# A state-space scan whose sums over states are issued one step later, with a guard on the order of the scans and a closed-up group of gelus

## The chip, the cores and the metric

The kernel runs on one core of one Trainium2 chip. The metric is the device time of one execution in microseconds; of several runs the median is taken. Smaller is better.

## The reference, cut to what matters

The kernel computes a chain of eight blocks over 2048 tokens of width 128 (8 sequences of 256), each followed by a layer norm. The change touches the stage that holds the second and third blocks: a local-attention layer (two sub-layers, each with attention and a gated feed-forward) and a selective state-space layer ("mamba") behind it. What it computes, for a sequence:

```
# gated feed-forward of a local sub-layer
h = h @ w1 + b1
a, g = split(h, 2)
x = x + (a * gelu(g)) @ w2 + b2

# state space: 256 inner channels, 16 states each
dA  = exp(delta[..., None] * A)                 # decay per step, channel and state
dBx = delta[..., None] * B[:, :, None, :] * xc[..., None]
h_t = dA_t * h_(t-1) + dBx_t                    # a scan along the 256 tokens
y_t = sum over the 16 states of h_t * C_t       # the sum over states
y   = (y + xc * D) * silu(z)
out = y @ W_out
```

## The kernel before, in words

Activations lie with channels on the 128 partitions and tokens along the free dimension. The method `local_mamba` holds the stage. Its work is written as Python generators, one for each sequence: `one_sequence` runs the two local sub-layers (`local_block`, with `local_attention` and `local_qk` inside), and `mamba_sequence` follows for the same sequence. A generator yields a number, its nominal length, and `interleave` always continues the one whose running sum is smallest. Four local sequences are open at a time, started 24 units apart; up to two mamba sequences run beside them, started at least 20 units apart. So the order in which the instructions are written down is a merge of up to six streams.

That order isn't yet the order on an engine. The framework that builds the program takes the place in the written order as a priority and lets each engine's next instruction be the one of highest priority among those that it reckons ready at that point. Whatever comes out is then fixed, and each engine takes its instructions in that order: in this trace TensorE stands idle for 42.9 us in front of sums over states that wait for VectorE, whatever is queued behind them. Two helpers bend the order: `issue_after` makes one instruction come behind another on the same engine, with no wait for its end; `wait_for` makes one wait for the end of another. `exp_ln` puts a load of the activation table for exp and ln behind the last activation written so far.

The steps that the change concerns:

- The scan (`mamba_sequence`, L776 to L793). A sequence has 8 steps, each with two of the 16 states. For each step, ScalarE makes the decay `da` by four exps (L785). VectorE multiplies `u` by the broadcast rows of B into `hs` (L787), scans (L789) and multiplies by the broadcast rows of C (L790). All three are 128x1024 in float32. Then TensorE adds the two states into the PSUM bank `yp` with two float32 matmuls of 128x512 against the identity (L792); a float32 matmul is two records in the profile, so a step has four. The program's name for `yp` is `y`. The buffers `hs` and `bc` (the broadcast rows, loaded by SyncE's queue, L754) have three slots each, `yp` has one.
- The end of a sequence (L794 to L802): VectorE reads `yp` (L796), GpSimd multiplies by silu(z) (L797; in the last sequence VectorE does), and TensorE applies `W_out`.
- The gate of the feed-forward (`local_block`, L685 to L694): three pairs of matmuls into the PSUM tiles `g`, then three gelus on ScalarE (L693), then `exp_ln`. Gelu lies in another activation table than exp and ln.
- The last sequence's mamba runs with other work woven in (`among`, `beside`): weight loads for the next stages, foldings of attention weights on TensorE (`fold`), and the routing of the next stage.

Of the kernel before, what the change touches and what calls it, by code (L numbers as in the profile page):

```python
# [15 lines left out]
AF = mybir.ActivationFunctionType  # L16
# [5 lines left out]
P = 128  # L22
# [274 lines left out]
class _Kernel:  # L297
    def __init__(self, ctx, tc, ins, out):
        self.tc, self.nc, self.ins, self.out = tc, tc.nc, ins, out
        nc = self.nc  # L300
        pool = lambda name, bufs=1, **kw: ctx.enter_context(tc.tile_pool(reuse_waits="tile", name=name, bufs=bufs, **kw))
        self.pool = pool


        self.right = lambda name, scope=ctx, bufs=1: scope.enter_context(
            tc.tile_pool(reuse_waits="tile", name=name, bufs=bufs, side="right")
        )
        self.const = const = pool("const")
        self.xs = pool("xs", 2)
        self.dram = pool("dram", space=DRAM)  # L310
        self.tags = {}


        self.chunk_scope = ctx.enter_context(ExitStack())
        self.tail = ctx.enter_context(ExitStack())
        self.scope = ctx.enter_context(ExitStack())
        n = ins["w0"].shape[1] // 2
        self.w0 = self.right("w0", self.scope).tile([P, 2, n], F32, name="w_local")
        self.x = self.xs.tile([P, T], F32, tag="x", name="x_in")
        nc.sync.dma_start(self.x, ins["x"])  # L320
        self.c12 = const.tile([P, 2], F32, name="c12")
        self.zero = const.tile([P, 1], F32, name="zero")
        nc.gpsimd.memset(self.zero, 0.0)
        self.one = const.tile([P, 1], F32, name="one")
        nc.gpsimd.memset(self.one, 1.0)
        self.wg = const.tile([P, 2, P], F32, name="wg")
        nc.sync.dma_start(self.wg, ins["wg"].rearrange("p (a b) -> p a b", a=2))
        self.vec = const.tile([P, _V["n"]], F32, name="vec")
        nc.sync.dma_start(self.vec, ins["vec"])
        self.rot = const.tile([P, 512], F32, name="rot_table")  # L330
        nc.sync.dma_start(self.rot, ins["cst"][:, slice(*_C["rot"])])
        r = slice(_C["iota32"][0], _C["n"])
        self.rt = const.tile([P, r.stop - r.start], F32, name="route_tables")
        nc.sync.dma_start(self.rt, ins["cst"][:, r])
        self.msk = const.tile([P, _M["n"]], BF, name="msk")
        nc.gpsimd.dma_start(self.msk, ins["msk"])
        self.ident = const.tile([P, P], F32, name="ident")
        make_identity(nc, self.ident)
        self.centre = const.tile([P, P], F32, name="centre")
        nc.vector.tensor_scalar(self.centre, self.ident, -1.0 / P, None, ALU.add)  # L340
        self.identb = const.tile([P, P], BF, name="identb")
        nc.vector.tensor_copy(self.identb, self.ident)
        self.mean = const.tile([P, P], F32, name="mean")
        nc.gpsimd.memset(self.mean, 1.0 / P)

        self.lg1 = [const.tile([P, n, 32], F32, name=f"lg1{n}") for n in (14, 2)]
        self.lg2 = const.tile([P, NT, 8], F32, name="lg2")
        self.ssq = const.tile([P, NT], F32, name="ssq")

        self.put1 = const.tile([P, NT], I32, name="put1")  # L350
        self.get1 = const.tile([P, NT], I32, name="get1")
        self.gate1 = const.tile([P, NT], F32, name="gate1")
        self.sum1 = const.tile([P, 32], BF, name="sum1")

        self.put2 = const.tile([P, 2, NT], I32, name="put2")
        self.get2 = const.tile([P, 2, NT], I32, name="get2")
        self.gate2 = const.tile([P, 2, NT], F32, name="gate2")
        self.sum2 = const.tile([P, 8], BF, name="sum2")
        self.onesb = const.tile([P, P], BF, name="onesb")
        nc.gpsimd.memset(self.onesb, 1.0)  # L360
        for l in range(2):
            nc.sync.dma_start(self.w0[:, l, :], ins["w0"][:, l * n : (l + 1) * n])
        self.w1 = const.tile([P, ins["w1"].shape[1]], F32, name="w1")
        nc.sync.dma_start(self.w1, ins["w1"])

        self.places = [self.dram.tile([2560, P], F32, name=f"places{i}") for i in range(2)]
        self.scatters = [], []
# [23 lines left out]
        return self.ps.tile([P, n], F32, tag=tag, name=name, bufs=self.tags[tag])  # L391

    def mm(self, out, lhsT, rhs, start=True, stop=True):
        return self.nc.tensor.matmul(out, lhsT, rhs, start=start, stop=stop)  # L394

    def issue_after(self, later, earlier):

# [268 lines left out]
    def local_block(self, l, x, w, rot, work, local, small, pools):  # L666

        nc = self.nc
        wo = w[:, l, 1536:2048].rearrange("p (c f) -> p c f", c=4)
        w1 = w[:, l, 2048:2730]  # L670
        w2 = w[:, l, 2730:3114].rearrange("p (c f) -> p c f", c=3)
        h = local.tile([P, S], F32, tag="h", name="h", bufs=3)
        self.shift(h, x)
        yield 1.0
        ot = yield from self.local_attention(l, h, w, rot, work, local, small, pools)
        ps = self.psum("M", "wo")
        for c in range(4):
            self.mm(ps[:, 0:S], wo[:, c, :], ot[:, c, :], c == 0, c == 3)
        x2 = local.tile([P, S], F32, tag="x2", name="x2", bufs=3)
        nc.vector.tensor_add(x2, ps[:, 0:S], x)  # L680
        h2 = work.tile([P, S], F32, tag="h2", name="h2")
        self.shift(h2, x2)
        yield 2.5
        self.layernorm(work, h2, h2)
        yield 4.5  # L685
        ge = local.tile([P, 3, S], F32, tag="ge", name="ge")
        size = lambda c: min(P, 341 - c * P)
        gs = [self.psum("M", "g") for _ in range(2)]
        part = lambda c: gs[c // 2][0 : size(c), c % 2 * S : (c % 2 + 1) * S]
        for c in range(3):  # L690
            self.mm(part(c), w1[:, 341 + c * P : 341 + c * P + size(c)], h2)
        for c in range(3):
            last = nc.scalar.activation(ge[0 : size(c), c, :], part(c), AF.Gelu, bias=self.v(f"b1g{l}", c)[0 : size(c), :])  # L693
        self.exp_ln(last)  # L694
        yield 4.0
        ps = self.psum("M", "a")
        for c in range(3):
            m = size(c)
            a = ps[0:m, c * S : (c + 1) * S] if c < 2 else gs[1][0:m, S : 2 * S]
            self.mm(a, w1[:, c * P : c * P + m], h2)  # L700
            nc.vector.scalar_tensor_tensor(ge[0:m, c, :], a, self.v(f"b1a{l}", c)[0:m, :], ge[0:m, c, :], ALU.add, ALU.mult)
        yield 2.0
        ps = self.psum("M", "w2")
        for c in range(3):
            m = size(c)
            self.mm(ps[:, 0:S], w2[0:m, c, :], ge[0:m, c, :], c == 0, c == 2)
        x3 = local.tile([P, S], F32, tag="x3", name="x3", bufs=3)
        nc.vector.scalar_tensor_tensor(x3, ps[:, 0:S], self.v(f"b2{l}"), x2, ALU.add, ALU.add)
        yield 1.5
        return x3  # L710


    def mamba_sequence(self, b, x, y, na, das, work, scan):


        nc = self.nc
# [56 lines left out]
        u = tile("u", 2)  # L773
        eng.tensor_mul(u, d, xc)  # L774
        yield 3.0
        yp = self.psum("Y", "y")  # L776
        shp = [P, 2, 2, S]
        for m in range(8):
            bc = rows(m)
            bn, cn = (bc[:, k].unsqueeze(2).to_broadcast(shp) for k in range(2))  # L780
            da = das[m % len(das)]
            for n in range(2):
                for c in range(2):
                    i = 16 * c + 2 * m + n
                    nc.scalar.activation(da[:, n, c, 1:S], d[:, c, 1:S], AF.Exp, scale=na[:, i : i + 1])  # L785
            hs = scan.tile(shp, F32, tag="hs", name="hs", bufs=3)
            nc.vector.tensor_tensor(hs, u.unsqueeze(1).to_broadcast(shp), bn, ALU.mult)  # L787
            line = lambda a: a.rearrange("p n c s -> p (n c s)")
            nc.vector.tensor_tensor_scan(line(hs), line(da), line(hs), 0.0, ALU.mult, ALU.add)  # L789
            nc.vector.tensor_tensor(hs, hs, cn, ALU.mult)  # L790
            for n in range(2):
                self.mm(yp, self.ident, flat(hs[:, n]), m == 0 and n == 0, m == 7 and n == 1)  # L792
            yield 2.3  # L793
        yg = tile("t")  # L794
        for c in range(2):
            nc.vector.scalar_tensor_tensor(yg[:, c, :], xc[:, c, :], self.v("dpar", c), yp[:, c * S : (c + 1) * S], ALU.mult, ALU.add)  # L796
        eng.tensor_mul(yg, yg, sz)  # L797
# [1015 lines left out]
```

## Time and profile before

| what | us |
|---|---|
| median of 3 runs | 1901.54 |
| lowest and highest | 1899.53, 1904.87 |
| the profiled execution: its time | 1852.0 |
| the profiled execution: its span | 1850.2 |
| mean granted TensorE clock in it | 0.929 |
| busy over the span: TensorE | 1557.4 (84%) |
| busy over the span: VectorE | 1095.6 (59%) |
| busy over the span: ScalarE | 1028.5 (56%) |
| busy over the span: GpSimd | 563.7 (30%) |

The first scan of the stage starts at 279.7 us and the last ends at 903.5 us; the stage's local attention begins before it, from about 100 us, and the next stage's gathers follow from about 925 us. The profile's rows give line, engine, operation, output and inputs by the program's names, the shape, the number of instructions, then busy time and mean duration in ns, and after the second bar the time that the engine stood idle just before these instructions, with what ended it. L394 is the helper that records all matmuls, so matmuls are told apart by their tiles. PE is TensorE, PEld its weight loads, DVE VectorE, ACT ScalarE, POOL GpSimd, SPq the queue of SyncE.

### The profile page before, as it was taken

To read this page: it belongs to the slowest core of one execution; us is meant where nothing else is said; L and a number is where in the kernel's file an instruction comes from. 1 tells how busy PE (TensorE), PEld (TensorE's weight loads), DVE (VectorE), ACT (ScalarE), POOL (GpSimd) and SP (SyncE) were. 2 spreads that over 40 slices of the span, in tenths; PEclk is the share of its full clock that TensorE was granted. 3 is DMA by queue.
4 is the path that set the end of the run, shared out by engine and by line. 5 is a ranking of instruction groups with operands and counts; after the bars stand their busy time and mean duration, and the time that the engine had idled before them with its cause. 6 is when DMAs were issued, how large, how long until landed. Compare 5 with 4: busy or idle time off the path is not lost.

```text
span 1850.2 us, 28438 instructions
## 1 busy us (share of the span) xinstructions
PE 1557.4 (84%) x10810; PEld 942.1 (51%) x10810; DVE 1095.6 (59%) x2016; ACT 1028.5 (56%) x2704; POOL 563.7 (30%) x493
## 2 busy tenths in 40 slices
PE   3668987878787867777579999999997999899997
PEld 2234543544454434344266766667663654465554
DVE  5734557777777776868714445557444223567664
ACT  4557776776777785566224454445443223465654
POOL 1324443433343323210511111111112025355552
PEclk7799998989998998788779999999998999899998
DMA  4000012111212121246440000000101311000000
GB/s 177 1 1 1 1 36 57 36 46 24 70 22 64 47 53 46 57 149 202 119 117 10 5 10 7 7 4 3 39 3 31 77 52 32 1 4 5 7 4 10
DMA packets 58330, 75.51 MB, mean 41 GB/s; under 512 B 5869, under 2 KB 35237, under 8 KB 57169
## 3 DMA queue, kind: packets, MB, share of 16 engines
q1 hardware_dynamic: 52864, 67.57, 12.8%
q0 software_dynamic: 3216, 5.07, 1.0%
q8 instruction: 85, 1.39, 0.3%
q10 hardware_dynamic: 2112, 1.05, 0.2%
q14 instruction: 53, 0.43, 0.1%
HBM read 65.46 MB, written 9.71 MB: 41 GB/s over the span
## 4 chain that ended last, share of the span: by engine, by line
PE 54%; DVE 19%; ACT 13%; issue 6%; POOL 6%; DMA 2%; POOLq 0%; DVEq 0%; SPq 0%; ACTq 0%
PE vps L394 7%; PE sc L394 7%; PE kps L394 6%; DVE hs L789 4%; PE out L394 4%; PE pt L475 4%; PE o L394 3%; PE pu L394 3%; PE pg L394 3%; ACT e L647 3%; DVE hs L790 2%; DVE hs L787 2%; PE y L394 2%; PE acc L394 2%; PE py L394 2%
## 5 line engine op out<-in xcount | busy, mean ns | idle before, releaser
L394 PE MATMUL y<-hs,ident 128*128 128x512 f32 x256 | 147.6, 706 | 42.9 <-DVE hs L790 42.8
L789 DVE TENSOR_TENSOR_SCAN hs<-da,hs 128x1024 f32<-128x1024 f32 x64 | 148.7, 2331 | 3.8 <-ACT da L785 3.3
L475 PE MATMUL pt<-ident,e 128*128 128x128 f32 x768 | 124.5, 288 | 28.2 <-POOL e L652 18.8
L1682 ACT ACTIVATE e<-sc,nm 128x128 f32<-128x128 f32 (+1 forms) x256 | 104.2, 424 | 59.3 <-DVE nm L1677 58.9
L652 POOL TENSOR_TENSOR e<-e,rc 128x1024 f32<-128x1024 f32 x32 | 72.2, 2255 | 204.6 <-DVE rc L651 204.5
L785 ACT ACTIVATE da<-d,na 128x255 f32<-128x255 f32 x256 | 112.1, 501 | 37.1 <-DVE hs L789 18.7
L1685 POOL TENSOR_TENSOR e<-e,rc 128x1024 f32<-128x1024 f32 x48 | 92.0, 1917 | 127.2 <-DVE rc L1684 94.2
L647 ACT ACTIVATE e<-sc,nm,rn 128x128 f32<-128x128 f32 x256 | 113.5, 464 | 25.2 <-DVE nm L642 25.0
L475 PEld LDWEIGHTS pt<-ident,e 128*128 128x128 f32 x768 | 89.2, 145 | 70.9 <-POOL e L652 25.4
L599 POOL TENSOR_TENSOR t<-t,t 128x512 f32<-128x512 f32 x64 | 89.1, 1392 | 96.5 <-DVE t L586 85.6
L1294 POOL TENSOR_TENSOR e<-e,rc 128x512 f32<-128x512 f32 x32 | 33.6, 1053 | 274.6 <-DVE rc L1293 160.3
L787 DVE TENSOR_TENSOR hs<-u,bc 128x1024 f32<-128x1024 f32 x64 | 86.6, 1362 | 43.2 <-POOL u L774 28.1
L394 PEld LDWEIGHTS y<-hs,ident 128*128 128x128 f32 x256 | 52.1, 219 | 98.9 <-DVE hs L790 55.7
L1269 ACT COPY kp<-kps 128x512 f32<-128x512 f32 x128 | 74.9, 585 | 42.2 <-PE kps L394 41.7
L477 ACT COPY ptsb<-pt 128x512 f32<-128x512 f32 x89 | 52.2, 587 | 82.4 <-PE pt L475 80.7
L1118 POOL DMA_INDIRECT got<-ybuf,get x48 | 45.7, 951 | 157.5 <-DMA ybuf<-ys 116.5
L394 PE MATMUL qk<-w_local,h 128*128 128x512 f32 x128 | 72.4, 653 | 17.6 <-DVE t L586 13.0
L477 DVE COPY ptsb<-pt 128x512 f32<-128x512 f32 x103 | 69.1, 685 | 29.8 <-PE pt L475 29.6
L790 DVE TENSOR_TENSOR hs<-hs,bc 128x1024 f32<-128x1024 f32 x64 | 81.8, 1286 | 0.2
L1677 DVE TENSOR_REDUCE nm<-sc 128x4 f32<-128x1024 f32 (+1 forms) x48 | 58.6, 1221 | 24.1 <-PE sc L394 23.9
L394 PE MATMUL sc<-km,q 64*128 64x512 f32 x192 | 69.9, 648 | 1.7 <-DVE FunctionType.Silu _12235 L1500 0.9
L1242 DVE BATCH_NORM_STATS2 st<-out 128x6 f32<-128x128 f32 x80 | 20.0, 288 | 81.0 <-PE out L394 74.0
(394 smaller groups left out, 3843.4 us busy)
## 6 DMA issues: line engine op xcount, KB each, us to landing
bc<-xs SPq DMA_DIRECT2D x128, 256.0 KB, 4.7
w_attn<-in_w_dram SPq DMA_DIRECT2D x4, 1024.0 KB
w_local<-in_w_dram SPq DMA_DIRECT2D x2, 1557.0 KB
places<-zeros SPq DMA_DIRECT2D x2, 1280.0 KB
w_moe<-in_e1gate_dram SPq DMA_DIRECT2D x8, 256.0 KB
w_moe<-in_e1up_dram SPq DMA_DIRECT2D x8, 256.0 KB, 7.5
w_moe<-in_e1down_dram SPq DMA_DIRECT2D x8, 256.0 KB, 5.3
w_moe<-in_e2rg_dram SPq DMA_DIRECT2D x8, 256.0 KB
```

What stands on the lines that cost most here:

```text
L394: return self.nc.tensor.matmul(out, lhsT, rhs, start=start, stop=stop)
L475: self.last = self.nc.tensor.transpose(pt[:, j * P : (j + 1) * P], src[:, j * P : (j + 1) * P], self.ident)
L477: self.nc.any.tensor_copy(sb.rearrange("p a b -> p (a b)"), pt)
L599: nc.gpsimd.tensor_add(t1, t1, t2)
L647: nc.scalar.activation(e[:, j, g, :], scs[:, j, g, :], AF.Exp, bias=nm[:, j, g : g + 1], scale=rq[:, j, g : g + 1], accum_out=sm[:, j, g : ...
L785: nc.scalar.activation(da[:, n, c, 1:S], d[:, c, 1:S], AF.Exp, scale=na[:, i : i + 1])
L787: nc.vector.tensor_tensor(hs, u.unsqueeze(1).to_broadcast(shp), bn, ALU.mult)
L789: nc.vector.tensor_tensor_scan(line(hs), line(da), line(hs), 0.0, ALU.mult, ALU.add)
L790: nc.vector.tensor_tensor(hs, hs, cn, ALU.mult)
L1269: nc.scalar.copy(k[:, 2 * i : 2 * i + 2, :].rearrange("p a b -> p (a b)"), ps)
L1682: nc.scalar.activation(e[:, i, :], sc[:, i, :], AF.Exp, bias=nm[:, i : i + 1], accum_out=sm[:, i : i + 1])
L1685: nc.gpsimd.tensor_tensor(e, e, rc.unsqueeze(2).to_broadcast([P, n, keys]), ALU.mult)
```

## The change

There are three edits.

1. The two summing matmuls of a step aren't written behind their own step. They are kept in a deque, and written after the following step's three VectorE instructions. Each is put behind the matmul that was written last before that point, by whichever stream (`self.pe_last`, which `mm` now records). The last step's sums come right after the loop. A step's nominal length becomes 2.5 in place of 2.3.
2. A guard: a sequence's scan doesn't begin to be written until the scan of the sequence before it is all written (`self.scanned`); until then the generator yields 0.5 at a time.
3. The three gelus are written at high priority, and the first of them waits for the end of the last of the three pairs of matmuls.

```diff
@@ __init__
+        self.scanned = 0
@@ mm
-        return self.nc.tensor.matmul(out, lhsT, rhs, start=start, stop=stop)
+        self.pe_last = self.nc.tensor.matmul(out, lhsT, rhs, start=start, stop=stop)
+        return self.pe_last
@@ local_block
         for c in range(3):
-            self.mm(part(c), w1[:, 341 + c * P : 341 + c * P + size(c)], h2)
-        for c in range(3):
-            last = nc.scalar.activation(ge[0 : size(c), c, :], part(c), AF.Gelu, bias=self.v(f"b1g{l}", c)[0 : size(c), :])
+            m = self.mm(part(c), w1[:, 341 + c * P : 341 + c * P + size(c)], h2)
+
+        with self.tc.high_priority():
+            for c in range(3):
+                last = nc.scalar.activation(ge[0 : size(c), c, :], part(c), AF.Gelu, bias=self.v(f"b1g{l}", c)[0 : size(c), :])
+                if c == 0:
+                    self.wait_for(last, m)
         self.exp_ln(last)
@@ mamba_sequence
+        while self.scanned < b:
+            yield 0.5
         yp = self.psum("Y", "y")
+        summed = deque()
+
+        def add(i, hs, last):
+
+            for n in range(2):
+                j = self.mm(yp, self.ident, flat(hs[:, n]), i == 0 and n == 0, i == 7 and n == 1)
+                self.issue_after([j], last)
@@ the loop over the 8 steps
             nc.vector.tensor_tensor_scan(line(hs), line(da), line(hs), 0.0, ALU.mult, ALU.add)
             nc.vector.tensor_tensor(hs, hs, cn, ALU.mult)
-            for n in range(2):
-                self.mm(yp, self.ident, flat(hs[:, n]), m == 0 and n == 0, m == 7 and n == 1)
-            yield 2.3
+            summed.append((m, hs))
+            last = self.pe_last
+            if m:
+                add(*summed.popleft(), last)
+            yield 2.5
+        add(*summed.popleft(), self.pe_last)
         yg = tile("t")
+        self.scanned = b + 1
```

## The prediction

> **What bounds the kernel now.** I read the busy time by stretches first: scans beside full local attention (280 to 760 us), the thinning end (760 to 850), the last scan nearly alone (850 to 910). Columns: length, busy us (instructions) of PE, PEld, DVE, ACT, POOL, then the granted PE clock, DMA share, GB/s.
>
> ```profile
> 280.00:760.00 480.00, 376.91 (x1955) 214.45 (x1955) 366.64 (x437) 354.50 (x872) 174.77 (x149) 0.93 0.20 48
> 760.00:850.00 90.00, 65.94 (x288) 37.70 (x290) 66.84 (x69) 43.73 (x98) 15.23 (x9) 0.83 0.44 138
> 850.00:910.00 60.00, 40.84 (x181) 21.40 (x179) 48.87 (x59) 27.83 (x61) 20.57 (x14) 0.83 0.56 171
> ```
>
> In the first stretch PE, DVE and ACT are 79%, 76% and 74% busy: none is full. They pass work to each other, so what counts is who stands waiting for whom. In the last, DVE is at 81% and leads. Next, the costliest groups of the page:
>
> ```profile
> L394 PE MATMUL y<-hs,ident 128*128 128x512 f32 x256 | 147.6, 706 | 42.9 <-DVE hs L790 42.8
> L789 DVE TENSOR_TENSOR_SCAN hs<-da,hs 128x1024 f32<-128x1024 f32 x64 | 148.7, 2331 | 3.8 <-ACT da L785 3.3
> ...
> L787 DVE TENSOR_TENSOR hs<-u,bc 128x1024 f32<-128x1024 f32 x64 | 86.6, 1362 | 43.2 <-POOL u L774 28.1
> ...
> L790 DVE TENSOR_TENSOR hs<-hs,bc 128x1024 f32<-128x1024 f32 x64 | 81.8, 1286 | 0.2
> ```
>
> The sums over states (y) make PE wait 42.9 us for the multiply by C (L790). A step costs DVE 2.33+1.36+1.29 = 4.98 us, 64 of them 319 us. PE's waits from 280 to 850 us, where other work is queued behind the sums:
>
> ```profile
> PE y L394 <- DVE hs L790: 31.2, 24, 3.5
> PE pt L475 <- POOL e L652: 14.5, 5, 7.9
> PE ln L394 <- POOL h L563: 11.8, 8, 2.2
> ```
>
> The sums are PE's largest wait; the other 11.7 us lie after 850, where PE has little else to do. Then the chain of waits, 280 to 800 us, its pieces of y:
>
> ```profile
> 316.46 3.78 PE y L394 x4
> ...
> 399.50 3.67 PE y L394 x4
> ...
> 578.14 3.78 PE y L394 x4
> 593.54 3.28 PE y L394 x4
> ```
>
> The same view gives DVE's three hs lines 12.1%, 7.0% and 5.8% of these 520 us, y 5.5%. So the chain runs through DVE's scans far more than through PE. Of the 24 waits it passes only five: by PE's timeline 2.65, 2.96, 3.31, 1.29 and (at 788.49) 0.22 us. Last, a gelu triple on ACT:
>
> ```profile
> 383.87 1.28 ACT L693 ACT_TABLE_LOAD   x1
> 385.17 0.47 ACT L693 ACTIVATE ge<-g,vec 128x256 f32<-128x256 f32 x1
> 385.66 1.28 ACT L593 ACT_TABLE_LOAD   x1
> 386.95 0.22 ACT L593 ACTIVATE rn<-rn 128x16 f32<-128x16 f32 x1
> 387.19 1.28 ACT L693 ACT_TABLE_LOAD   x1
> 388.48 0.47 ACT L693 ACTIVATE ge<-g,vec 128x256 f32<-128x256 f32 x1
> ```
>
> An exp slips between two gelus, and the table is loaded twice more. L693 has 22 loads for 16 triples: six such splits, 12 extra loads.
>
> **What the Trainium skill says.** "TensorE: Matmul & The Clock Gate", in the section on the array's 16 sub-arrays: PE can pull weight loads ahead, but matmuls start strictly in order. The trace agrees: a waiting y leaves PE idle whatever is behind it. The same page, Part 1, says that the clock halves after an idle window; here a y matmul takes 592 ns as a median and 1222 at most. "ScalarE: Activation LUTs", What ACT_TABLE_LOAD costs: 1283 ns and about 1380 ns of drain. The trace has the 1283 ns; the next activation follows within 0.02 us, and the load starts 0.02 us after the gelu, so I count no drain. "DVE: opcode table, instruction layouts, handler registers and perf-mode slots", Datapath: a scan runs at half throughput; here 2331 ns against 1286 for a multiply of that size. The change leaves that cost alone.
>
> **The sums one step later.** Nothing is removed: 256 matmuls and their weight loads stay. The moved step issues no DMA and passes no queue but PE's; `bc` is released by L790, so SP's loads are untouched. A sum now comes behind the matmul written last before the following step's position. Steps stand about 7.1 us apart (in the third sequence 472.1 to 528.9 us, 8 steps), so hs is normally finished. All 31.2 us of waits can go at most. I credit what the chain passes: 2.65+2.96+3.31+1.29+0.22 = 10.4 us. The others end in slack: the chain at those times is in DVE, whose queue still carries 4.98 us a step. The four long groups shown also run at the slow clock: 3.78+3.67+3.78+3.28 less 4 x 1.98 (the group at 788.49) is 6.6 us. A sum that follows running work should be warm, but the next wait may cool other matmuls: I take half, 3.3, with ends 0 and 6.6. After 850 us the wait isn't credited: DVE is late next. The last sum of a sequence still comes straight after its multiply, so the final `t` waits as now (3.71 us in the last sequence). The 2.5 in place of 2.3 gives each step a slightly lower priority against the local streams: unknown, see the noise below.
>
> **The guard.** By adding up the yields: mamba sequences begin 23 or 24 units apart, a scan starts 8 units in and lasts 8 x 2.5 = 20, so it is over (28) before the next one's starts (31). No 0.5 is ever yielded. The trace agrees: the first sequence's last scan starts at 331.9 us, the second's first at 376.4. Cost and gain nothing; there is no cover that could go.
>
> **The gelus.** High priority and the common start close the six splits: 12 x 1.283 = 15.4 us of ACT. On the chain lies one, the one shown: 2 x 1.283 = 2.6 us. The others are behind ACT's slack. The added wait: the first gelu holds ACT's queue (exps of attention and of `da`, whose waiters are DVE's) until the third pair of g. Four matmul records took 1.03 us at 482.99, so 16 triples cost 0 to 16 us. I take 0: the order is laid out with the gelus when g should be ready, and the last gelu is no later than now. Below zero it can't go, apart from the loads already counted.
>
> **Noise of the order.** Every shift re-sorts the queues. From 629 to 658 us, a silu placed behind the combined exp/ln table cost a row of single loads (L592, L593, L766, L785, L439 among them), some 11 until the table returned at 674.9: 14 us of ACT. Another order may lose or repeat it: minus 14 to plus 14, taken as 0.
>
> **Sum.** 10.4 + 3.3 + 2.6 = 16.3 us off the profiled execution's 1852.0, 0.88%. The median of the runs shown is 2.7% above that execution, so I scale: 1901.5 x (1 - 16.3/1852.0) = 1884.8, say 1885.
>
> **Rivals.** *All of it counts:* 31.2 + 15.4 = 46.6 us, 1901.5 x (1 - 46.6/1852) = 1853.7. For it: the three engines are equally loaded, so each stall may come back. Against: five of 24 waits on the chain.
>
> *Nothing comes of it:* DVE's queue holds everything, and PE merely waits elsewhere: 1901.5. For it: 25% of the chain is hs on DVE. Against: DVE itself waits 57.9 us for PE between 280 and 850.
>
> *Slower, by the slots of hs:* there are three, and the multiply by B (L787) of step m needs the sum of step m-3 done. That now ends later in PE's order. I took each sum's end (less its wait) one step later and compared it with the end of the multiply by C before the step in need: of 40 cases the median slack is 3.8 us, three are short, by 13.2 us together. If PE runs another 2 us behind, 13 are short, by 26.6; at 3 us 18, by 41.8. The loss overtakes the gain of 16.3 at about 0.5 us beyond a full step. At 2 us: 26.6 - 16.3 = 10.3 more, 1901.5 x (1 + 10.3/1852) = 1912. For it: only 2.3 us of L787's waits are on y now, but often just 2 us after the slot came free. Against: a sum can go a step late at most where PE is that far behind the written order.
>
> **Chances.** The forecast 0.52, all of it 0.16, nothing 0.10, slower 0.22. About 0.3% (5.7 us) is what a measurement can tell from no change. Faster 0.68, same 0.10, slower 0.22. The forecast alone, with its bounds (clock, gelu wait, noise), spans 1868 to 1900. The range reaches into both outer cases: 1855 to 1912, leaving out half of each.
>
> **What would show it.** Right: y's wait on L790 between 280 and 850 us falls under 8 us; L693 has 16 loads; first and last scans keep their order; L787 waits little for y. The last scan (867 to 905) keeps its length. Wrong: L787 idle for y by over 15 us (slots), PE's total idle unchanged with other names on it (nothing), or new rows of table loads.

## The result and the profile after

| | before | after |
|---|---|---|
| median us (7 runs each) | 1903.64 | 1916.57 |
| ratio, 95% interval | | 1.0072 [1.0057, 1.0086] |
| profiled execution, its span in us | 1850.2 | 1917.0 |
| start of the first scan, us | 279.7 | 285.9 |
| end of the last sum over states, us | 908.4 | 921.7 |
| PE idle for sums, whole span, us | 42.9 | 29.5 |
| loads of activation tables before 930 us | 77 | 63 |

The kernel became 0.7% slower. The two spans can't be subtracted: by all signs they come from different chips. On chips 6, 13 and 14 the kernel before took 1848 to 1850 us as a median, on chips 3 and 7 1900 to 1902; the part behind the last sum, the same code in both, took 941.8 us in the profile of before and 995.3 in that of after. So I compare these two traces only up to the end of the last sum, where after is 13.3 us later, close to the 12.9 us between the medians. Of the 13.3 us, 6.2 lie before the first scan. The ratios of the experiments are against the kernel before on the same chip.

The same stretches and the groups of the page, after:

```profile
280.00:760.00 480.00, 380.41 (x1952) 220.41 (x1953) 351.47 (x427) 329.94 (x835) 170.47 (x149) 0.91 0.16 45
760.00:850.00 90.00, 65.26 (x258) 34.86 (x256) 69.08 (x69) 53.47 (x130) 11.46 (x9) 0.82 0.36 110
850.00:910.00 60.00, 43.39 (x217) 24.27 (x216) 52.00 (x62) 31.66 (x67) 4.62 (x3) 0.84 0.61 189
```

```profile
L395 PE MATMUL y<-hs,ident 128*128 128x512 f32 x256 | 141.7, 680 | 29.5 <-DVE hs L805 29.3
L804 DVE TENSOR_TENSOR_SCAN hs<-da,hs 128x1024 f32<-128x1024 f32 x64 | 149.8, 2346 | 1.2 <-ACT da L800 1.0
...
L802 DVE TENSOR_TENSOR hs<-u,bc 128x1024 f32<-128x1024 f32 x64 | 80.2, 1262 | 45.5 <-POOL u L780 27.3
...
L805 DVE TENSOR_TENSOR hs<-hs,bc 128x1024 f32<-128x1024 f32 x64 | 86.9, 1365 | 0.2
```

PE waits less for the sums and is a little busier from 280 to 760 us, yet DVE does less in that time (351 against 367 us). ACT's 330 against 355 us are for the most part 16 table loads fewer (37 against 53, 20.5 us). Over 280 to 850 us, PE's busy time is 445.7 us against 442.9: its idle time hardly changed, and other names stand on it. PE's waits and DVE's waits for sums, 280 to 850 us, after:

```profile
PE y L395 <- DVE hs L805: 16.7, 9, 5.7
PE sc L395 <- ACT e L649: 12.0, 8, 6.0
PE lg L395 <- DVE x_mamba L443: 10.3, 4, 3.7
```
```profile
DVE hs L802 <- PE y L395: 12.1, 8, 4.0
DVE t L815 <- PE y L395: 11.1, 6, 3.6
```

The same waits of DVE before:

```profile
DVE t L796 <- PE y L394: 8.3, 4, 3.8
DVE hs L787 <- PE y L394: 2.3, 1, 2.3
```

Where 31.2 us of PE's waits were to vanish, 14.5 did, and DVE now waits 23.2 us for late sums (10.6 before: 2.3 for slots of hs, 8.3 at the ends of sequences). From the end of the multiply by C to the end of its sum took 2.7 us as a median over the first six sequences before, 11.3 after, 25.4 at most; a step takes 6.7 us after, as a median. The lag grows within a sequence: 4.5 us for its first step, 19.7 for its last (medians of the six).

What it costs shows at the end of a sequence. PE's timeline at the end of the first one, first before, lines of other tiles left out:

```profile
339.86 1.88 PE L394 MATMUL y<-hs,ident 128*128 128x512 f32 x4
...
350.19 1.15 PE L394 MATMUL o<-ptsb,v 128*64 128x64 f32 x30
...
352.19 1.03 PE L394 MATMUL z<-x_local,w 128*128 128x256 f32 x4
...
353.72 1.13 PE L394 MATMUL wout<-t,w 128*128 128x256 f32 x4
```

The silu product was ready long before wout's turn came, at 345.66 us:

```profile
344.40 1.26 POOL L797 TENSOR_TENSOR t<-t,sz 128x512 f32<-128x512 f32 x1
```

The same place after:

```profile
366.03 1.15 PE L395 MATMUL o<-ptsb,v 128*64 128x64 f32 x30 [0.42 <-ACT ptsb L479]
367.11 1.98 PE L395 MATMUL y<-hs,ident 128*128 128x512 f32 x4
...
371.41 1.13 PE L395 MATMUL wout<-t,w 128*128 128x256 f32 x4 [0.49 <-POOL t L816]
372.47 1.05 PE L395 MATMUL xps<-xc,w 128*33 128x256 f32 x4
...
374.04 0.69 PE L395 MATMUL raw<-xs,ident 33*128 33x256 f32 x2
374.66 1.56 PE L395 MATMUL wo<-ot,w_local 128*128 128x256 f32 x6
```

In the timelines of the other engines, the input of xps (the next sequence's xc), and what lies between that sum and wout:

```profile
354.16 0.63 ACT L744 ACTIVATE xc<-xc 128x512 f32<-128x512 f32 x1
...
369.13 0.87 DVE L815 SCALAR_TENSOR_TENSOR t<-xc,vec,y 128x256 f32<-128x256 f32 x2 [1.93 <-PE y L395]
...
370.08 1.28 POOL L816 TENSOR_TENSOR t<-t,sz 128x512 f32<-128x512 f32 x1 [2.06 <-DVE t L815]
```

The last sum could run from 344.4 us, when its multiply by C ended; it runs at 367.11, right behind the attention output o. That o is the matmul of another stream that was written last when the sum was written, and PE reached it only 22 us after the sum was ready. Then t, the silu product and wout follow, and o, wout, xps, raw and wo all take their PSUM room from the two banks with the tag M. Between o and wout (367.18 to 371.41 us) no M matmul starts, though the input of xps was there from 354.79. For these 4.2 us no stream gets an M bank for a new tile. I measured this gap ahead of wout for the first six sequences: 0.5, 1.8, 0.4, 1.4, 0.1 and none before, 4.2, 4.5, 4.4, 4.2, 4.5 and 4.1 after. The next sequence pays: in the second, third and fourth sequence xps came 17.7, 10.5 and 9.9 us after its input, against 4.1, 2.7 and 5.1 before. The tiles at the very end of a sequence have their turn among the M tiles too: PE's wait ahead of lg, 10.3 us above, was 0.5 before.

The reason lies in the program. In the instruction list of before, each of the stage's 202 tiles of tag M gets its first matmul in exactly the order written, without one exception; so do the tiles of the other PSUM tags, and in the changed kernel and its variants that leave wout in M it is the same. A tile that is written later never overtakes one of the same tag. The end of a sequence thus has a fixed turn among the local streams' matmuls, and the forced place of the last sum puts sum, t, silu product and wout all into that turn.

### The profile page after: what moved, and what is told of

The parts are those of the page before. It is cut to its first block, busy times and chain, and to the rows that moved or that the text cites. A ratio compares the mean times of both kernels' runs of the same rounds, so it can differ in the third digit from the quotient of the medians.

```text
span 1917.0 us, 28426 instructions
## 1 busy us (share of the span) xinstructions
PE 1590.2 (83%) x10810; PEld 958.5 (50%) x10810; DVE 1089.3 (57%) x2010; ACT 1016.4 (53%) x2697; POOL 548.7 (29%) x493
## 4 chain that ended last, share of the span: by engine, by line
PE 56%; DVE 18%; ACT 10%; issue 6%; POOL 6%; another core or an unknown queue 2%; DMA 1%; POOLq 0%; SPq 0%; DVEq 0%; ACTq 0%
PE vps L395 7%; PE sc L395 7%; PE kps L395 6%; PE pt L477 4%; PE out L395 4%; PE o L395 4%; PE pu L395 3%; PE pg L395 3%; DVE hs L804 3%; ACT e L649 2%; DVE hs L805 2%; DVE hs L802 2%; PE y L395 2%; PE hps L395 2%
## 5 line engine op out<-in xcount | busy, mean ns | idle before, releaser
L395 PE MATMUL y<-hs,ident 128*128 128x512 f32 x256 | 141.7, 680 | 29.5 <-DVE hs L805 29.3
L477 PE MATMUL pt<-ident,e 128*128 128x128 f32 x768 | 127.1, 293 | 25.4 <-POOL e L654 13.4
L477 PEld LDWEIGHTS pt<-ident,e 128*128 128x128 f32 x768 | 91.7, 148 | 74.2 <-issue 23.2
L802 DVE TENSOR_TENSOR hs<-u,bc 128x1024 f32<-128x1024 f32 x64 | 80.2, 1262 | 45.5 <-POOL u L780 27.3
L805 DVE TENSOR_TENSOR hs<-hs,bc 128x1024 f32<-128x1024 f32 x64 | 86.9, 1365 | 0.2
L479 DVE COPY ptsb<-pt 128x512 f32<-128x512 f32 x97 | 65.0, 685 | 30.2 <-PE pt L477 29.9
L1696 DVE TENSOR_REDUCE nm<-sc 128x4 f32<-128x1024 f32 (+1 forms) x48 | 58.6, 1220 | 25.4 <-PE sc L395 25.1
L395 PE MATMUL sc<-msk,identb 128*128 128x512 bf16 (+2 forms) x224 | 53.5, 366 | 23.2 <-ACT e L649 23.2
```

Of the source, the lines that this page charges most:

```text
L395: self.pe_last = self.nc.tensor.matmul(out, lhsT, rhs, start=start, stop=stop)
L477: self.last = self.nc.tensor.transpose(pt[:, j * P : (j + 1) * P], src[:, j * P : (j + 1) * P], self.ident)
L479: self.nc.any.tensor_copy(sb.rearrange("p a b -> p (a b)"), pt)
```

## The experiments

**The kernel before once more.**

> The kernel before once more, for a second profile beside the first (span 1850.2 us, first scan at 279.7 us, last sum over at 908.4 us), because the stages behind the last sum, whose code is the same in both kernels, took 941.8 us in the first profile of before and 995.3 us in that of after. If the first profile caught a quick execution, this one has about 1895 to 1905 us with the last sum still at 905 to 912 us; if the stage of the scans itself was quick in it, the last sum comes at 915 us or later.

1848.41 us, first scan at 282.5 us, last sum over at 911.2, the part behind it 935.5. The stage is the same as in the first profile (2.8 us later at the first scan and at the last sum); and 1848 us isn't a lucky execution but that chip's usual time. My bound of 1895 to 1905 us was that of another chip.

**The guard** needed no run: without it the instruction lists of all five engines are the same.

**The gelus alone, the sums alone, and the changed kernel without the forced place.** For the second, the gelu edit and the guard are taken back. For the third:

```diff
-                self.issue_after([j], last)
```

> The gelu edit alone (high priority, the first gelu waits for the last pair of matmuls), the sums as before. Theory of the sums (the late sums lose the time): about the time before, 1895 to 1905 us, with 16 gelu loads. Rival of the gelus (they cut into other sequences' exps and hold ScalarE before the first scan, which came 6.2 us later in after): 6 to 13 us over before, 1909 to 1917 us, first scan at 284 us or later.

0.9987 [0.9979, 0.9995], 1846.99 us. The scans did start later, by 5.8 us in the first sequence (288.3 us against 282.5 on the same chip) and 10.7 in the third, but 3.8 in the sixth and 3.4 earlier in the seventh. The gelus have their 16 loads, but three exps of the attention, cut off by a triple, load their own table: `exp_ln` isn't at high priority. In the changed kernel seven do.

> The sums one step later with their place in the order and the length of 2.5; no gelu edit, no guard. Theory of the sums: the whole loss, 1912 to 1918 us, VectorE waiting 10 us or more for sums to free the slots of hs. Rival of the gelus: within 3 us of before, or under it, 1885 to 1906 us.

1.0075 [1.0057, 1.0092], 1863.69 us. PE waits less for sums than before (28.4 against 42.1 us over the whole span), and DVE waits 10.6 us for slots and 10.0 for t (280 to 865 us). The whole loss is here.

> The changed kernel, but the delayed sums aren't put behind the matmul written last; they keep only their later place in the written order. Theory of the sums, with the forced place as the cause: sums follow their multiply within some us again, and the time falls to before or under it, 1885 to 1905 us. If the later written place is enough to lose: 1910 us or more, as after. Rival of the gelus: 1909 to 1917 us.

0.9938 [0.9920, 0.9956], 1836.52 us. So the forced place loses, not the later written one. A look at its waits of PE, 100 to 905 us, first this kernel, then the kernel before on the same chip:

```profile
PE y L395 <- DVE hs L804: 47.2, 28, 5.7
```
```profile
PE y L394 <- DVE hs L790: 39.7, 27, 4.0
```

It is the faster one, and its PE waits longer for sums. So it isn't a shorter wait that makes it faster.

**Delay and forced place one by one, and the slots of hs.** All four start from `sums_alone`.

```diff
# later_nopin: sums_alone without the forced place
-                self.issue_after([j], last)
# pin_own_step: the forced place without the delay
-            if m:
-                add(*summed.popleft(), last)
+            add(*summed.popleft(), last)
-        add(*summed.popleft(), self.pe_last)
# cut_hs3: room for the next one
-x3 and x_local bufs=3, xs bufs=2
+x3 and x_local bufs=2, xs bufs=1
# cut_hs4: as cut_hs3, and
-            hs = scan.tile(shp, F32, tag="hs", name="hs", bufs=3)
+            hs = scan.tile(shp, F32, tag="hs", name="hs", bufs=4)
```

> The sums written one step later and the length of 2.5, without the forced place behind the matmul written last; gelus as before, no guard. Theory of the forced place: 0.990 to 1.000 of before, the sums end 3 to 5 us after their multiply (median). Rival, that the later written place loses and the gelu edit made up for it in the run with both: 1.003 or more.

0.9912 [0.9894, 0.9929]; lag 5.1 us as a median over the first six sequences, just above the expected 3 to 5. Here PE's wait for sums fell (26.9 us over the whole span), and the time too.

> The sums written in their own step as before, but put behind the matmul written last before that step (the forced place without the delay); length 2.5, gelus as before. Theory that only both together are late enough to lose: 0.995 to 1.003 of before, the sums' median lag under 4 us. Rival, that any forced place behind other streams' matmuls loses: 1.004 or more.

0.9944 [0.9925, 0.9963], lag 3.9 us: it gains against the kernel before. But it also has the length of 2.5, which alone gives 0.9907 (`pace25_alone`, below); against that kernel the forced place costs 0.4%. So a forced place by itself loses too, less than with the delay.

> The delayed and forced sums (the kernel that gave 1.0075), with one slot less of each of x_local, x3 and xs: the mate of the next run, which needs that room. 1.004 to 1.012 of before in every theory; if the slots taken away matter by themselves, more.

1.0090 [1.0072, 1.0108].

> The same with four slots of hs in place of three. Theory of the slots (VectorE's multiply by B waits for a late sum to free one): at least half of the loss goes, 1.000 to 1.004 of before, with under 3 us of waits of that multiply for sums. Rival, that the late sums lose by holding back other work on TensorE or the end of each sequence: within 0.002 of the mate with three.

1.0081 [1.0060, 1.0102]. In the three-slot mate the multiply by B waits 9.0 us for sums; with four slots that wait is gone from the list, and the time stays. My theory of the slots, the rival of the prediction and my own at this point, falls. The gap of 4 us and more ahead of wout is in both (4.2 to 5.2 us, and 4.1 to 5.2). From it came the theory of the M banks.

**Which sums, and wout out of the M banks.** The `pin_` kernels and `sums_wout_y` start from `sums_alone`, the other two from `later_nopin` and from the changed kernel.

```diff
# pin_first5: i < 5; pin_last3: i >= 5; pin_only7: i == 7
-                self.issue_after([j], last)
+                if i < 5:
+                    self.issue_after([j], last)
# sums_wout_y, later_nopin_wout_y, after_wout_y
-        ps = self.psum("M", "wout")[:, 0:S]
+        ps = self.psum("Y", "wout")[:, 0:S]
```

> The delayed sums, with the forced place only for steps 0 to 4; the last three, which the end of the sequence waits for, go free. New theory, of the M banks: matmuls that use the two PSUM banks M start strictly in the order written; the end of a sequence (wout) has its place among them, and a forced last sum makes all later ones wait some 4.3 us for sum, t, silu product and wout. Then freeing the last sums recovers most: 0.990 to 1.000 of before, M idle under 1.5 us ahead of wout. Rival, that the early sums lose it (by order or slots): 1.005 to 1.009, as with all forced.

0.9973 [0.9960, 0.9987]. The gaps ahead of wout: none, 0.3, 2.2, none, 4.5, 3.2 us, the last two above the 1.5 us expected. Against the free sums (0.9912) the five forced ones still cost 0.6%.

> The mirror: the forced place only for steps 5 to 7. Theory of the M banks: the loss stays, 1.004 to 1.010 of before, M idle 4 us or more ahead of each of the first six wout. Rival of the early sums: 0.990 to 1.000.

1.0070 [1.0053, 1.0088], gaps of 4.1 to 4.8 us. Forcing the last three sums is enough for nearly the whole loss.

> All sums delayed and forced, as in the run that gave 1.0075, but the output product wout takes its PSUM room from the bank of the sums, not from the two M banks, so nothing of the other streams has its turn behind it. Theory of the M banks: 7 ends of some 4.3 us no longer hold the streams, at least two thirds of the loss goes: 0.985 to 1.002 of before. Rival, that late sums delay the next sequence through other waits (the tile t, the order of TensorE): 1.004 to 1.009.

0.9974 [0.9959, 0.9989]. The sums end as late as ever (last sums 22.4, 22.3, 17.1 and 24.3 us after their multiply in the first four sequences), but no other M tile has its turn behind wout; the gaps are 0.2 to 1.9 us, and xps comes 6.2, 5.1 and 3.8 us after its input in the second to fourth sequence. PE's timeline at the end of the first sequence:

```profile
359.23 0.81 PE L395 MATMUL xps<-xc,w 128*33 128x256 f32 x3
...
361.00 1.99 PE L395 MATMUL y<-hs,ident 128*128 128x512 f32 x4
362.92 0.69 PE L395 MATMUL raw<-xs,ident 33*128 33x256 f32 x2
363.54 1.56 PE L395 MATMUL wo<-ot,w_local 128*128 128x256 f32 x6
365.30 1.13 PE L395 MATMUL wout<-t,w 128*128 128x256 f32 x4 [0.20 <-POOL t L810]
```

xps, raw and wo, which stood behind wout in the changed kernel, pass it here.

> The best run so far (sums later, not forced, 0.9912) with wout in the bank of the sums. Theory of the M banks: little is left to gain, since M stood idle under 0.5 us ahead of most wout; 0.985 to 0.993 of before. If the end of a sequence costs more than that idle time shows: under 0.985.

0.9908 [0.9891, 0.9924]: as expected, nothing more to gain where the gaps are small. So the move of wout is worth nothing by itself here; on the kernel before it was not tried alone.

> The changed kernel as it is, gelu edit and all, with the output product's PSUM room moved from the two M banks to the bank of the sums. Theory of the M banks: the loss of 1.0072 is gone, 0.990 to 1.001. Rival, that in the full change something else loses (gelus cutting into exps, order): 1.004 or more.

1.0001 [0.9989, 1.0014]. One bank's name takes the loss of 0.72% out of the changed kernel itself, gelus and all, and not by way of table loads (62 against 63 before 930 us). Against the changed kernel without the forced place (0.9938) 0.6% are still lost.

> All sums one step later, only the last one of each sequence put behind the matmul written last. Theory of the M banks in its narrowest form: this one place carries the loss, 1.003 to 1.010 of before, M idle 4 us or more ahead of most wout. If the steps 5 and 6 are needed too: under 1.000.

0.9994 [0.9981, 1.0007]. This is the second of the two cases: steps 5 and 6 are needed too. Its gaps are 4.1 to 5.0 us, as large as with three sums forced, and xps is as late (16.6, 9.9 and 9.9 us), but against the free sums (0.9912) it loses 0.8% and not 1.6%. So the length of the gap doesn't give the size of the loss alone; what steps 5 and 6 add is open.

**Where a gain comes from.**

```diff
# pace25_alone (on the kernel before)
-            yield 2.3
+            yield 2.5
# later_nopin_23: later_nopin with yield 2.3
# before_silu (on the kernel before)
-        nc.scalar.activation(flat(sz), ps, AF.Silu)
-        self.exp_ln(nc.scalar.activation(xc, xc, AF.Silu))
+        silu = nc.scalar.activation(flat(sz), ps, AF.Silu)
+        self.issue_after([self.exp_ln(nc.scalar.activation(xc, xc, AF.Silu))], silu)
```

> The kernel before with a step's nominal length of 2.5 in place of 2.3, nothing else. If the gain of the free later sums (0.9912) is the later sums' own: 0.997 to 1.003 of before. If it comes from the length, which lowers the scans' priority against the local streams: 0.988 to 0.995.

0.9907 [0.9891, 0.9924], with the sums as before. The length alone gains as much as the free later sums with it.

> The sums written one step later and not forced, with the old length of 2.3. If the gain is the later sums' own: 0.988 to 0.995 of before. If it comes from the length: 0.997 to 1.003.

0.9878 [0.9857, 0.9898], the fastest kernel here, with PE waiting 48.5 us for sums over the whole span. Either edit gains about 1% by itself, and the two together no more than one (0.9912).

> The kernel before, with the load of the exp/ln table put behind both silus of a sequence in place of the second alone; the order of the engines changes little else. It takes away the row of single table loads from 632 to 674 us. If that row is what every re-sorted kernel here gained by losing it (0.9907 with the length of 2.5 alone): 0.990 to 0.995 of before. If a table load there lies beside other work, as I assumed when I took it at nothing: 0.998 to 1.001.

0.9977 [0.9965, 0.9988]: between my two bounds, with the second one inside the interval. The eight single loads from 635 to 658 us are gone, and 70 loads are left of 77 before 930 us. This row costs about a quarter of what the re-sorted kernels gain.

**The slots again, with the M banks out of the way.** `cut_hs4` with wout in the bank of the sums.

> All sums delayed and forced, wout in the bank of the sums, and four slots of hs (one slot less of x_local, x3 and xs). With three slots and wout in that bank it was 0.9974, with free sums 0.9908. If the slots make the rest, now that the M banks are out of the way: 0.990 to 0.994. If not: 0.996 to 1.000.

0.9996 [0.9977, 1.0015]. A fourth slot doesn't bring the rest back either. No run has three slots with the same room taken away and wout moved; in `cut_hs3` that room cost 0.15%, within the noise. Against `cut_hs4` (1.0081) the move of wout brought 0.85%: a third pair, after the sums alone and the changed kernel, with the same sign and about the same size.

## Why the prediction was wrong

The forecast was 16.7 us less; measured are 12.9 us more.

- **The sums one step later: wrong, and here the sum failed.** That hs is "normally finished" one step later was beside the point. (The 7.1 us between steps are a mean with one hole of 22.6 us in it; the median of the first six sequences was 5.9.) I priced where a sum would no longer wait, and never where its new place would put it. The sentence that let it through is that the last sum "still comes straight after its multiply, so the final `t` waits as now": it too is put behind `pe_last`, a matmul of another stream that PE reaches much later, and it ended 24.7 us after its multiply in the first sequence (5.4 before). DVE's wait for t rose from 8.3 to 11.1 us, the small part; the large part is the M banks' turn behind wout. Shown: moving wout out of M takes the changed kernel from 1.0072 to 1.0001, and the sums alone from 1.0075 to 0.9974, with the sums about as late as before. Every edit also sorts the order anew, which alone can be worth 0.9%; but three pairs gained 0.7 to 1.0% by the move of wout, and the pair with free sums nothing. Of the forced place's whole cost that is 1.0 of 1.6% with the sums alone (0.9912 to 1.0075), and 0.7 of 1.3% in the changed kernel (0.9938 to 1.0072).
- **The 10.4 us credited for waits on the chain: not supported.** With the sums alone, PE's waits fell and the time rose; in three kernels without the forced place the time fell, whether the waits rose (`after_nopin`, `later_nopin_23`) or fell (`later_nopin`). A gain of that size and more does appear when the sums are later and free, but the length of 2.5 alone gives it too, so it can't be booked to those waits. The 3.3 us for the clock came true for the sums themselves, which took 144.4 us in `sums_alone` against 148.6 on the same chip, and brought no time.
- **The guard: right.** Inert, down to the last instruction.
- **The gelus: right in size, in part by luck.** 2.6 us forecast, 2.4 measured (0.9987 of 1849, interval 0.9 to 3.9 us). The loads of L693 fell from 22 to 16. But the first scan came 5.8 us later and the last sum 3.2 us earlier; that this comes from the one split on the chain isn't shown. What else I didn't see is that a triple at high priority, with its table load behind it at ordinary priority, leaves room for exps in between; seven extra loads in the changed kernel.
- **The noise of the order: taken at nothing, and it is no noise.** The row of table loads is an event of this one order. The changed kernel lost it, and so did the sums alone (2 loads from 625 to 680 us against 18); without it before gains 0.23%. (Of the eleven loads that I counted, those of L439 and L440 at 667.89 and 671.37 us lie inside a gelu triple and stay.) Three quarters of the 0.9% that the length brings are open.
- **The slots: a rival with the right sign and the wrong mechanism.** It gave 1912 us, near the result. L802's wait for sums rose to 12.1 us as it said, but four slots don't bring the time back (1.0081 against 1.0090). I had stopped at the first wait that lengthens.
- **Of the signs to look for,** y's wait under 8 us was wrong (16.7), L693's 16 loads right, "L787 idle for y by over 15 us" not reached. The last scan didn't keep its length: 39.1 us against 36.4. The sign of the rival "nothing", PE's total idle unchanged with other names on it, did appear (124.3 us against 127.2 from 280 to 850), though the time did not stay the same. "All of it counts" had the wrong sign.
- **A place in the Trainium skill:** that matmuls start strictly in order stands on the page named, "TensorE: Matmul & The Clock Gate", in Part 3, The mechanism, and not in the section on the sub-arrays, which has the weight loads alone.

Open: what makes the 0.7% between sums_wout_y and later_nopin_wout_y. DVE waits 20.2 us for the sum at t (L809) in the one and 2.6 in the other, from 280 to 865 us; it fits in size, but I have not tried it by itself. A rival is untested: lg, and the last ln of a sequence, are still M tiles that come behind the late sum (PE waits 4.5 us ahead of lg in the one, 2.8 in the other). Open too is the larger part of what the length of 2.5 gains.

## What to carry to other kernels

Before pricing a wait that an edit removes, ask which place in every queue the moved instruction gets, and which shared room its consumers take: a chain that ends in a PSUM bank handed out in written order holds every stream that uses the bank. The longest wait of the busiest engine may lie in slack. Here it halved while the time rose, so look for the wait that stands ahead of shared things, and move the consumer to another bank before moving the producer. Where a scheduler sorts the order, an edit should be judged beside a neutral shift of about the same size (here a length of 2.5 in place of 2.3, worth 0.9%).

## What the runs showed of the hardware that I had not expected

The kernel before takes 1848 to 1850 us on three of the chips and 1900 to 1902 on two. The difference lies in the stages behind the scans: their part took 935.2 to 943.7 us in twelve profiles on chips 6, 13 and 14, and 987.4 to 995.5 in six on chips 3 and 7, with the same code. From 930 to 1840 us the mean granted clock was 0.98 on chip 14 (kernel before) and 0.95 on chip 7 (the kernel with the silu edit); why the chips differ is open. The first profile's 941.8 us fit the faster chips, and so the 2.7% by which I scaled the profiled execution to the median were most likely this, and no property of the kernel.
